# Layer 2 of a four-layer graph kernel: weight[l] w_ih^T multiplied out once per launch, and the state transposed at each step

**Chip, cores, metric.** One core of one Trainium2 chip.

## The reference, cut to what matters

64 graphs of 256 nodes with 256 features go through four layers. Each takes relu(layernorm(x)), and its result is added to x. Layer 0 is attention over 8 heads, layer 1 attention over one, layer 3 over four; layer 2 is a gated graph network of three steps with one pair of GRU matrices for all of them:

```python
A = (adj != 0).astype(x.dtype)
h = x                                             # relu(layernorm(x))
for i in range(3):
    m = einsum('bnd,de->bne', h, weight[i])       # 256 x 256
    aggr = einsum('bst,bsd->btd', A, m)           # A^T m
    gi = aggr @ w_ih.T + b_ih                     # 256 x 768
    gh = h @ w_hh.T + b_hh
    r = sigmoid(i_r + h_r); z = sigmoid(i_z + h_z)
    n = tanh(i_n + r * h_n)
    h = (1 - z) * n + z * h
```

Since aggr w_ih^T = A^T h (weight[i] w_ih^T), the product of the two matrices can be made once, and the multiplication by weight[i] goes out of the steps.

## The kernel before

All is in fp32. Two graphs, a pair, go through all layers together; up to three pairs are under way, some steps apart, so that one's matrix products fill another's softmax. A kernel line that says `yield` ends a step. The code's matmuls sum over the tiles' first axis, so there are two layouts: "T" tiles (features on partitions) and "token" tiles (nodes on partitions). The state hT is a T tile. psgm = h weight[l] makes a token tile m out of it, as a side effect of the multiplication:

```python
def layer2(xt, at, p):
    am = mask(f"am_{p}")
    ...
    hT = yield from norm_relu_T(xt, f"2_{p}")     # psn: transposes; then relu on ScalarE
    yield
    for l in range(NL):
        psm, psm4 = token_ps(f"psgm_{nm}")
        token_mm(gg_sb[:, l], hT, psm4)           # 8 matmuls of 128x256
        m = w4(f"m_{nm}")
        nc.scalar.copy(m, psm)
        yield
        psa = ...                                 # A^T m, 8 matmuls of 128x256
        aT = w4T(f"aT_{nm}")
        nc.scalar.copy(aT, psa)
        yield
        both = ((whhT, hT), (wihT, aT))
        r = sigmoid(0, "r")                       # psr: 8 matmuls of 128x512
        pshn = gate(((whhT, hT),), 4, "pshn")
        ...
        psin = gate(((wihT, aT),), 4, "psin")
        ...
        yield
        z = sigmoid(2, "z")                       # psz
        hnew = ...                                # named hg: n + z (h - n), GpSimd and VectorE
        hT = hnew
        yield
    ps, ps4 = token_ps(f"psx_{p}")                # psx: state to tokens, added to x
    for t in range(T):
        for k in range(2):
            nc.tensor.transpose(ps4[t][:, k*P:(k+1)*P], hT[:, k, t*P:(t+1)*P], ident)
    nc.vector.tensor_add(xt, ps, xt)
    yield
```

In layer 1, psf and psw are its projections, e its softmax numerators, wh the projected values divided by the sums, and psh<-wh,e the product of the two. psc and pso<-f,eT are the products of the softmaxes in layers 0 and 3.

## Time and profile before

| | before |
|---|---|
| time, median | 6370.52 us (3 runs, 6350.54 to 6373.97) |
| TensorE busy | 5787.0 us of 6365.3, 91% |
| TensorE idle | 578 us |
| mean granted clock of TensorE | 0.890 |
| a round (three pairs), mean of nine | 587.5 us |

The work repeats in rounds of three pairs, 10.67 of them. Slices, groups and one round of the timeline stand in the prediction. What TensorE waits for is in the view of its waits (tile, line, what it waited for: us in all, times, longest us); four of its lines:

```profile
PE psc L341 <- DVE pT L334: 143.6, 97, 4.7
PE psx L520 <- DVE hg L514: 88.9, 22, 6.8
PE psn L241 <- DVE xn L234: 44.6, 12, 5.2
PE psh L427 <- DVE wh L421: 18.7, 10, 6.6
```

psx waits long, twice in a round, for the new state hg. psh, the product of layer 1, hardly waits.

### The profile page before, as it was taken

The numbers are of one execution on the slowest core, as the hardware profiler recorded it, in microseconds if no ns is written. First come the engines' busy times: TensorE is split into PE (matmuls) and PEld (weight loads), VectorE is DVE, ScalarE is ACT, GpSimd is POOL, SyncE is SP. The second block draws the span as 40 slices with busy tenths as digits, with TensorE's granted clock in tenths as the row PEclk, the third lists the DMA queues.
The fourth block names the chain that finished last, engine by engine and source line by source line (L and its number), as shares of the span: only waits on it lengthen the run. The fifth ranks groups of instructions, "written<-read, shape, count | busy, mean of one in ns | idle before, by whom it ended". The sixth has DMA issues, their size and how long they took to land.

```text
span 6365.3 us, 60565 instructions
## 1 busy us (share of the span) xinstructions
PE 5787.0 (91%) x24500; PEld 3967.9 (62%) x24500; DVE 3090.6 (49%) x4479; ACT 2004.0 (31%) x4737; POOL 777.0 (12%) x582
## 2 busy tenths in 40 slices
PE   7998899889989988998899889889988998999887
PEld 6655765666566556655765665576557656665755
DVE  4435534554454445445544553554455345534534
ACT  2323322332233233223322332242233223322422
POOL 1011101100110111011001101110110011001011
PEclk7899799889978997898899889978987998899798
DMA  1000000000000000000000000000000000000000
GB/s 53 1 4 19 9 1 7 17 7 1 14 17 1 4 14 14 1 4 20 7 1 14 17 1 4 14 14 1 4 20 7 1 7 17 7 1 10 7 0 7
DMA packets 58279, 58.40 MB, mean 9 GB/s; under 512 B 4752, under 2 KB 58000, under 8 KB 58000
## 3 DMA queue, kind: packets, MB, share of 16 engines
q1 hardware_dynamic: 58000, 54.54, 2.6%
q8 instruction: 192, 3.15, 0.2%
q14 instruction: 87, 0.71, 0.0%
HBM read 37.76 MB, written 16.78 MB: 9 GB/s over the span
## 4 chain that ended last, share of the span: by engine, by line
PE 78%; DVE 13%; ACT 8%; issue 1%; DMA 0%; POOL 0%; SPq 0%; ACTq 0%; POOLq 0%; DVEq 0%
PE psr L475 10%; PE psz L475 10%; PE psc L341 9%; PE psin L475 5%; PE pshn L475 5%; PE psa L457 5%; PE pso L580 5%; PE psgm L250 4%; PE pssd L548 3%; PE pss L300 3%; DVE mx L260 3%; PE psq L278 2%; ACT s L262 2%; PE pso L250 2%; PE psf L536 2%; ACT eT L574 2%
## 5 line engine op out<-in xcount | busy, mean ns | idle before, releaser
L341 PE MATMUL psc<-v,pT 128*128 128x32 f32 x4096 | 621.6, 316 | 146.1 <-DVE pT L334 143.6
L341 PEld LDWEIGHTS psc<-v,pT 128*128 128x128 f32 x4096 | 612.1, 237 | 198.7 <-DVE pT L334 92.6
L262 ACT ACTIVATE s<-s,mx 128x256 f32<-128x256 f32 x1024 | 506.8, 499 | 304.5 <-DVE mx L260 166.0
L262 ACT ACTIVATE e<-e,mx 128x256 f32<-128x256 f32 x640 | 318.0, 500 | 630.6 <-DVE mx L260 630.5
L580 PE MATMUL pso<-f,eT 128*128 128x64 f32 x2048 | 323.1, 324 | 193.6 <-ACT eT L574 193.5
L580 PEld LDWEIGHTS pso<-f,eT 128*128 128x128 f32 x2048 | 302.8, 234 | 228.9 <-ACT eT L574 228.9
L307 DVE SCALAR_TENSOR_TENSOR s<-pss,mb 128x1024 f32<-128x1024 f32 x256 | 306.8, 1219 | 176.4 <-PE pss L300 176.4
L457 PE MATMUL psa<-am,m 128*128 128x256 f32 x1536 | 369.5, 396 | 2.3 <-ACT m L451 2.2
L475 PE MATMUL psz<-aT,wihT 128*128 128x512 f32 x768 | 363.6, 596 | 0.0
L475 PE MATMUL psr<-aT,wihT 128*128 128x512 f32 x768 | 363.3, 593 | 0.0
L475 PE MATMUL psin<-aT,wihT 128*128 128x512 f32 x768 | 345.2, 592 | 0.0
L457 PEld LDWEIGHTS psa<-am,m 128*128 128x128 f32 x1536 | 298.8, 199 | 47.6 <-ACT m L451 7.2
L327 PE MATMUL pst<-ident,s 128*128 128x128 f32 x2048 | 297.7, 307 | 18.7 <-DVE pT L334 14.5
L494 DVE TENSOR_SCALAR z<-z 128x1024 f32<-128x1024 f32 x96 | 66.6, 693 | 493.9 <-ACT z L491 493.9
L327 PEld LDWEIGHTS pst<-ident,s 128*128 128x128 f32 x2048 | 278.2, 163 | 32.8 <-DVE pT L334 17.1
L260 DVE TENSOR_REDUCE mx<-s 128x8 f32<-128x2048 f32 x128 | 292.0, 2281 | 1.2
L243 ACT ACTIVATE hT<-psn 128x1024 f32<-128x1024 f32 x128 | 130.9, 1022 | 488.8 <-PE psn L241 488.7
L348 DVE TENSOR_TENSOR ctxs<-psc,rz 128x256 f32<-128x256 f32 x128 | 54.4, 425 | 459.7 <-PE psc L341 459.7
L230 POOL TENSOR_SCALAR rs<-mv 128x4 f32<-128x4 f32 x128 | 33.7, 263 | 1973.1 <-DVE mv L228 1730.7
L475 PEld LDWEIGHTS psz<-aT,wihT 128*128 128x128 f32 x768 | 148.6, 194 | 191.0 <-issue 191.0
L250 PE MATMUL psgm<-gg_sb,hg 128*128 128x256 f32 x1024 | 254.4, 405 | 14.4 <-DVE hg L514 14.4
L594 POOL TENSOR_TENSOR x<-o,x 128x256 f32<-128x256 f32 x128 | 118.9, 929 | 1177.9 <-DVE o L588 1164.4
(140 smaller groups left out, 10040.8 us busy)
## 6 DMA issues: line engine op xcount, KB each, us to landing
x<-in_x_dram SPq DMA_DIRECT2D x32, 512.0 KB, 3.4
adj<-in_adj_dram SPq DMA_DIRECT2D x32, 512.0 KB, 3.3
out_dram<-x SPq DMA_DIRECT2D x32, 512.0 KB, 2.9
gg_sb<-in_L_gnn_weight_dram SPq DMA_DIRECT2D x3, 256.0 KB, 6.3
wih_sb<-in_L_gnn_w_ih_dram SPq DMA_DIRECT2D x1, 768.0 KB, 6.4
whh_sb<-in_L_gnn_w_hh_dram SPq DMA_DIRECT2D x1, 768.0 KB, 7.2
wq_sb<-in_L_gnn_Wq_dram SPq DMA_DIRECT2D x1, 256.0 KB, 5.4
wk_sb<-in_L_gnn_Wk_dram SPq DMA_DIRECT2D x1, 256.0 KB, 5.6
```

The costliest lines, as they stand in the source:

```text
L243: nc.scalar.activation(hT, ps, AF.Relu)
L250: mm(ps4[t], hT[:, k, t * P : (t + 1) * P], rhs[:, k, :], start=k == 0, stop=k == 1)
L260: nc.vector.tensor_reduce(mx, e, AX.X, ALU.max, negate=True)
L262: nc.scalar.activation(e[:, i, :], e[:, i, :], AF.Exp, bias=mx[:, i : i + 1], accum_out=zs[:, i : i + 1])
L300: mm(ps[:, j, cc * N : (cc + 1) * N], qT[r : r + D0, cc, t * P : (t + 1) * P], kT[r : r + D0, cc, g * N : (g + 1) * N], start=True, stop=True,
L307: nc.vector.scalar_tensor_tensor(s[:, 4 * half : 4 * half + 4, :], ps.rearrange("p a (b d) -> p (a b) d", d=N), SCALE, mb0[:, t : t + 1, : ...
L327: nc.tensor.transpose(psr[:, 2 * i + c, :], s[:, 4 * half + i, c * P : (c + 1) * P], ident)
L341: mm(ps[:, 0, h * D0 : (h + 1) * D0], pT[:, i, c, :], v[:, 2 * g + c, h * D0 : (h + 1) * D0], start=c == 0, stop=c == 1,)
L457: mm(psa[:, o, g * N : (g + 1) * N], m[:, 2 * g + c, o * P : (o + 1) * P], am[:, 2 * g + c, :], start=c == 0, stop=c == 1,)
L475: mm(ps[:, o, :], w[:, k, c0 : c0 + P], src[:, k, :], start=n == 0, stop=n == 2 * len(terms) - 1,)
L548: mm(ps[:, j, :], wdst_bc[:, k, 2 * half + j, :], hT[:, k, :], start=k == 0, stop=k == 1)
L580: mm(pso[:, 0, h * C3 : (h + 1) * C3], eT[:, 2 * h + c, :], f[:, 2 * g + c, h * C3 : (h + 1) * C3], start=c == 0, stop=c == 1,)
```

## The change

Its intent is to take 96 groups of psgm from TensorE, the engine that bounds the kernel, and to pay with 64 groups of transposes, which at full clock take 0.88 us each in the trace before, where a psgm takes 3.45. The first step of a pair needs none: the layernorm's tile is a token tile already and gets its relu in place. Cut to its core (removed comments, buffer lines and helper functions are left out):

```diff
+        for l in range(NL):                      # once per launch
+            transposed(ggT, gg_sb[:, l], D)
+            ... giT[:, l] = weight[l] @ w_ih.T
     def w4(name):
-        ... bufs=17
+        ... bufs=16
     def mask(name):
-        ... bufs=2
+        ... bufs=3
     def norm_relu_T(xt, nm, both=False):
+        if both:
+            nc.vector.tensor_scalar_max(xn, xn, 0.0)
         yield
         ...
-        return hT
+        return (hT, xn) if both else hT
     def layer2(xt, at, p):
-        hT = yield from norm_relu_T(xt, f"2_{p}")
+        hT, h = yield from norm_relu_T(xt, f"2_{p}", both=True)
         for l in range(NL):
-            psm, psm4 = token_ps(f"psgm_{nm}")
-            token_mm(gg_sb[:, l], hT, psm4)
-            m = w4(f"m_{nm}")
-            nc.scalar.copy(m, psm)
-            yield
-                            m[:, 2 * g + c, o * P : (o + 1) * P],
+                            h[:, 2 * g + c, o * P : (o + 1) * P],
-            both = ((whhT, hT), (wihT, aT))
+            both = ((whhT, hT), (giT[:, l], aT))
             ...
             hT = hnew
             yield
+            if l < NL - 1:
+                ps, ps4 = token_ps(f"psh2_{nm}")
+                to_tokens(hT, ps4)
+                h = w4(f"h_{nm}")
+                nc.scalar.copy(h, ps)
+                yield
```

The profile shows psh2 as psh<-ident,hg; psh<-wh,e is the product of layer 1.

More of the change, by code (lines that the diff above doesn't have):

```diff
@@ L98, in tile_adj_preln_d4 @@
     wo_sb = load_w("wo_sb", wo)
-    gg_sb = const.tile([P, NL, 2, D], FP, name="gg_sb")
-    for l in range(NL):
-        nc.sync.dma_start(gg_sb[:, l], ggw[l].rearrange("(k p) o -> p k o", p=P))
     def row_bcast(dst, vec):
@@ L117, in tile_adj_preln_d4 @@
     row_bcast(b3a_bc[:, 0:D], b3)
-    wihT = const.tile([P, 2, 3 * D], FP, name="wihT")
+    giT = const.tile([P, NL, 2, 3 * D], FP, name="giT")
     whhT = const.tile([P, 2, 3 * D], FP, name="whhT")
@@ L142, in transposed @@
                     nc.vector.tensor_copy(dst[:, k, o * P : (o + m) * P], ps[:, 0, 0 : m * P])
+        gg_sb = prep.tile([P, NL, 2, D], FP, name="gg_sb")
+        for l in range(NL):
+            nc.sync.dma_start(gg_sb[:, l], ggw[l].rearrange("(k p) o -> p k o", p=P))
+        wihT = prep.tile([P, 2, 3 * D], FP, name="wihT")
         for w, wT, nm in ((w_ih, wihT, "wih_sb"), (w_hh, whhT, "whh_sb")):
@@ L147, in tile_adj_preln_d4 @@
             transposed(wT, t, 3 * D)
+        HALF = 3 * D // 2
+        for l in range(NL):
+            ggT = prep.tile([P, 2, D], FP, tag="ggT", bufs=2, name=f"ggT_{l}")
+            transposed(ggT, gg_sb[:, l], D)
+            for f in range(2):
+                ps = bank2(f"gi_{l}_{f}")
+                for half in range(2):
+                    for k in range(2):
+                        mm(
+                            ps[:, half, 0:HALF],
+                            ggT[:, k, f * P : (f + 1) * P],
+                            wihT[:, k, half * HALF : (half + 1) * HALF],
+                            start=k == 0,
+                            stop=k == 1,
+                        )
+                nc.scalar.copy(giT[:, l, f, :].rearrange("p (h e) -> p h e", h=2), ps[:, :, 0:HALF])
         nc.vector.tensor_add(brz, bih_sb[:, 0:4], bhh_sb[:, 0:4])
@@ L208, in w4 @@
     def w4(name):
-        return work.tile([P, T, D], FP, tag="w4", bufs=17, name=name)
+        return work.tile([P, T, D], FP, tag="w4", bufs=16, name=name)
     def w4T(name):
@@ L218, in mask, with to_T, to_tokens, norm_relu_T @@
     def mask(name):
-        return work.tile([P, T, N], FP, tag="mask", bufs=2, name=name)
-    def norm_relu_T(xt, nm):
+        return work.tile([P, T, N], FP, tag="mask", bufs=3, name=name)
+    def to_T(src, ps):
+        for k in range(2):
+            for t in range(T):
+                nc.tensor.transpose(ps[:, k, t * P : (t + 1) * P], src[:, t, k * P : (k + 1) * P], ident)
+    def to_tokens(src, ps4):
+        for t in range(T):
+            for k in range(2):
+                nc.tensor.transpose(ps4[t][:, k * P : (k + 1) * P], src[:, k, t * P : (t + 1) * P], ident)
+    def norm_relu_T(xt, nm, both=False):
         st = small.tile([P, T, 6], FP, tag="st", name=f"st_{nm}")
@@ L236, in norm_relu_T @@
             )
+        if both:
+            nc.vector.tensor_scalar_max(xn, xn, 0.0)
         yield
         ps = bank2(f"psn_{nm}")
-        for k in range(2):
-            for t in range(T):
-                nc.tensor.transpose(ps[:, k, t * P : (t + 1) * P], xn[:, t, k * P : (k + 1) * P], ident)
+        to_T(xn, ps)
         hT = work.tile([P, 2, N2], FP, tag="hT", bufs=4, name=f"hT_{nm}")
         nc.scalar.activation(hT, ps, AF.Relu)
-        return hT
+        return (hT, xn) if both else hT
     def token_mm(rhs, hT, ps4):
@@ L503, in layer2 @@
                 )
-            psin = gate(((wihT, aT),), 4, "psin")
+            psin = gate(((giT[:, l], aT),), 4, "psin")
             nc.vector.tensor_add(hn, psin, hn)
@@ L516, in layer2 @@
             yield
+            if l < NL - 1:
[4 more added lines that the diff above has]
+                yield
         ps, ps4 = token_ps(f"psx_{p}")
-        for t in range(T):
-            for k in range(2):
-                nc.tensor.transpose(ps4[t][:, k * P : (k + 1) * P], hT[:, k, t * P : (t + 1) * P], ident)
+        to_tokens(hT, ps4)
         nc.vector.tensor_add(xt, ps, xt)
```

## The prediction

> **What bounds the kernel now.** I read the page first: busy times, slices, chain of waits.
>
> ```profile
> PE 5787.0 (91%) x24500; PEld 3967.9 (62%) x24500; DVE 3090.6 (49%) x4479; ACT 2004.0 (31%) x4737; POOL 777.0 (12%) x582
> PEclk7899799889978997898899889978987998899798
> PE 78%; DVE 13%; ACT 8%; issue 1%; DMA 0%; POOL 0%; SPq 0%; ACTq 0%; POOLq 0%; DVEq 0%
> ```
>
> TensorE bounds the kernel, and 78% of the chain that ended last is TensorE work. But 13% of its 91% lies beside someone else's link of the chain: removing such work gives nothing. The clock dips to 0.7 once in every round of three pairs of graphs (some 587 us: the third psx of a round starts at 1167.9, that of the next at 1754.7). Then the groups of TensorE by shape:
>
> ```profile
> L250 PE MATMUL psgm<-gg_sb,hg 128*128 128x256 f32 x1024 | 254.4, 405 | 14.4 <-DVE hg L514 14.4
> L250 PE MATMUL psgm<-gg_sb,hT 128*128 128x256 f32 x512 | 138.8, 433 | 0.0
> L520 PE MATMUL psx<-ident,hg 128*128 128x128 f32 x256 | 43.4, 325 | 88.9 <-DVE hg L514 88.9
> ```
>
> psgm is what goes: 254.4 + 138.8 = 393.2 us busy. psx is the same sort of transposes that come: 43.4 / 256 = 0.17 us each. Each psgm matmul shows as two records, each transpose as one. In the chain of waits psgm has 4.0% of the span, 255 us, so about a third of psgm is already hidden. Last, the timeline of TensorE in one round (start, length; idle before it in brackets):
>
> ```profile
> 970.71 1.88 PE L475 MATMUL psz<-aT,wihT 128*128 128x512 f32 x4
> 972.43 3.62 PE L250 MATMUL psgm<-gg_sb,hg 128*128 128x256 f32 x16
> 975.88 3.62 PE L427 MATMUL psh<-wh,e 128*128 128x256 f32 x16
> 979.33 1.04 PE L520 MATMUL psx<-ident,hg 128*128 128x128 f32 x8
> ...
> 1075.71 3.62 PE L250 MATMUL psgm<-gg_sb,hg 128*128 128x256 f32 x16
> 1080.64 1.06 PE L520 MATMUL psx<-ident,hg 128*128 128x128 f32 x8 [1.31 <-DVE hg L514]
> ...
> 1167.89 1.94 PE L520 MATMUL psx<-ident,hg 128*128 128x128 f32 x8 [6.78 <-DVE hg L514]
> 1169.62 1.91 PE L241 MATMUL psn<-ident,xn 128*128 128x128 f32 x8
> ```
>
> Around 972, psgm fills the time in which layer 1's softmax is made for psh: no wait. At 1075.71 it fills most of the 4.9 us that z and the new state take on ScalarE and VectorE: only 1.31 us remain. At 1167.89 nothing fills: 6.78 us idle[...].
>
> [...]after 6.78 us idle 8 transposes take 1.9 us, against 1.04 elsewhere, and the next psq 6.28 us where psk of the same size takes 3.60. [...]Full clock: 16 psgm records 3.45 us, 8 transposes 0.88 us, so a factor of 3.9 for as many output elements[...] Of the same shape, z<-z takes 0.693 us and the tensor_tensor hg 1.22[...]the new maximum should cost 0.69 us.
>
> **The change, part by part.** There are 32 pairs, 10.67 rounds.
> *TensorE:* out go 96 psgm, 393 us. In come 2 × 32 × 8 = 512 transposes, 512 × 0.17 = 87 us. Busy time falls by 306 us: were the idle time unchanged, 6370 - 306 = 6064.
> *Preparation:* 12 transposes and 24 matmuls of 128x384. The same kind at full clock: psr, 8 matmuls of 128x512, takes 6.87 us, so 24 × 0.86 × 0.75 = 15.5; transposes 1.6; waits for copies between them some 4. 21 us, all before the first psn, so all on the path.
> *Other engines:* VectorE gets 32 × 0.69 = 22 us; ScalarE loses 32 of 96 copies of 1.01 us. A third mask buffer frees VectorE from waits on psa (97.6 + 80.2 us), but these fall into stretches in which TensorE is full, so I count nothing. DMA moves the same weights.
>
> *Where the wait moves.* I compiled the changed kernel and read the order of instructions, without times. I then put the durations of the trace on one round:
>
> a) From psc before the round's first psgm (805.1) to the second step's psr (884.0). The first psgm goes; psa moves into the wait for layer 1's softmax. The new transposes stand right behind psz, psn and pss and wait some 2.6 us for the state. Layer 1's psh is ready at 865.8 as against 866.5 (bounded by VectorE), but 4.7 us of psa no longer stand behind it: gain 5.6 us.
> b) psr at 884.0 to psr at 925.3: psgm 3.45 and psgm 3.69 with its wait of 1.31 go, one set of transposes 0.9 and a wait of 0.6 come; psm moves out (0.9), psct in (counted in a): gain 6.2.
> c) To psr at 983.8. Psh now stands behind psf, psw, psx, psa, no more behind psz and psgm. From the end of psw, VectorE does half of e, x, e, e, mx with statistics between, ScalarE 2.1 us of exponentials, VectorE rz and wh: 10.3 us. TensorE has psx 0.9 and psa 3.45 to do: it waits 6.0 us where it waited 0. Sum of the pieces: 63 us against 58.5: loss 4.5.
> d) To psr at 1030.4: psgm 3.45 goes, another becomes transposes (3.45 - 0.9): gain 5.9.
> e) To psr at 1089.2: before psx at 1080.64 only 0.9 us of transposes remain as cover, and VectorE's order now puts two passes over e between z and the new state, 2.45 us: psx comes at 1083, after 6.5 us idle: loss 2.5.
> f) The psgm at 1125: 3.45 - 0.9: gain 2.55.
>
> Sum 5.6 + 6.2 - 4.5 + 5.9 - 2.5 + 2.55 = 13.3 us a round. [...]after the one at 1167.89 about 3 us of matmul were lost. I count 2 + 3 + 1 = 6 us a round. That leaves 7 to 13 us a round, 75 to 140 us, less 21 for preparation: a gain of 55 to 120 us. By the busy time it would be 285.
>
> **Rivals.**
> 1. *The whole 306 us come through, less preparation: 6085.* For it: TensorE is 91% busy, 100% between 925 and 984. Against it: the chain shows a third of psgm hidden, which caps the gain at 255 - 45 - 21, or 190 us (6180).
> 2. *The removed psgm was cover; new waits at psh and psx and a halved clock eat it: 6250 to 6315.* For it: the compiled order, and the wait of 6.78 us at 1167.89, which is what psx without cover looks like. Against it: I placed the pieces by hand; 2 us at one place of the round shift the sum by 21.
> 3. *VectorE becomes the bound or clocks fall in the dense stretch too: 6350 or more.* VectorE is at 49% and gets 22 us; transposes already stand among dense matmuls (psn at 997.40, 16 in 1.91 us, full clock). Unlikely.
>
> **Range and chances.** Mostly rival 2, with some weight on rival 1 capped by the chain: 6275 us, 6170 to 6360 eight times in ten. The line of 2% lies at 6243, between the cap (6180) and my middle: faster 0.35, same 0.62, slower 0.03.
>
> **What would show it.** Psgm gone; new transposes 70 to 90 us busy; TensorE about 5500 us busy, more if the clock halves oftener; its share of the span falling to 87 or 88%. In the waits: psh for wh up from 18.7 us to 60 to 100, psx for hg from 88.9 to 130 to 145, a new wait of the state's transposes for hg of about 30. Slow psh or psa behind those waits, mean clock at or below 0.89. First psn at 50 us in place of 29.4. I am wrong if psh and psx wait no longer than before (then 6100 to 6200), or if the round of 587 us shrinks by over 15 us.

Passages that no trace of this case shows are cut from it, and marked. A gain of 13.3 us a round, less 6 for the clock, is 7.3, taken as 7 to 13 (from the whole clock term to none); in 10.67 rounds and less 21 us of preparation that gave the gain of 55 to 120 us. The 6 us are my estimate. It starts from the about 3 us that I put down as lost at 1167.89, after 6.78 us idle, where psx took 1.94 us in place of 1.04 and the next psq 6.28 where psk took 3.60 (granted clock 0.50 and 0.57), and carries that over to the waits of 6.0 us in c), 6.5 in e) and 3.9 in a) as 2, 3 and 1 us; that such a loss follows waits of these lengths is an assumption. The 0.69 us of the new maximum is the measured length of z<-z, of the same shape.

## More of the kernel before

The metric is the device time of one execution in microseconds (us), as the median of the runs.

In which order TensorE gets the matmuls of the three pairs is set when the kernel is compiled: a scheduler arranges the steps' instructions, and the source gives only a part of that order.

## The result

| | before | after |
|---|---|---|
| time, median of 4 runs | 6366.73 us (6350.54 to 6373.97) | 6389.67 us (6387.44 to 6393.66) |
| ratio | | 1.0048, 95% interval 1.0029 to 1.0067 |
| TensorE busy | 5787.0 us | 5630.3 us |
| TensorE idle | 578 us | 755 us |
| mean granted clock | 0.890 | 0.867 |
| first psn starts at | 29.43 us | 48.60 us |
| a round, mean of nine | 587.5 us | 589.0 us |

A ratio here and below is the mean time of one kernel's fast runs over that of the other's fast runs of the same rounds, so it is not quite the ratio of the medians quoted. The time lies above the predicted range, and it is slightly slower: the interval leaves out 1. The changed kernel is correct.

From the page after: busy times and the chain of waits.

```profile
PE 5630.3 (88%) x23536; PEld 3818.6 (60%) x23536; DVE 3115.1 (49%) x4517; ACT 1974.8 (31%) x4711; POOL 793.8 (12%) x582
PE 77%; DVE 13%; ACT 7%; issue 1%; POOL 0%; DMA 0%; SPq 0%; ACTq 0%; POOLq 0%; DVEq 0%
```

The groups by shape (busy us, mean ns | idle us just before), and the waits:

```profile
L457 PE MATMUL psh<-wh,e 128*128 128x256 f32 x512 | 167.6, 499 | 113.7 <-DVE wh L451 113.7
L249 PE MATMUL psh<-ident,hg 128*128 128x128 f32 x512 | 76.8, 300 | 50.2 <-DVE hg L539 50.2
L249 PE MATMUL psx<-ident,hg 128*128 128x128 f32 x256 | 53.1, 377 | 136.8 <-DVE hg L539 136.8
```

```profile
PE psx L249 <- DVE hg L539: 136.8, 22, 6.8
PE psc L371 <- DVE pT L364: 115.3, 97, 4.5
PE psh L457 <- DVE wh L451: 113.7, 22, 6.6
PE psn L243 <- DVE xn L268: 78.8, 11, 7.8
PE psh L249 <- DVE hg L539: 50.2, 22, 3.9
```

psgm is gone, 393.2 us of it. The new transposes take 76.8 us, the products in the preparation 16.2 and its 12 transposes about 2, so busy time should have fallen by 298 us. It fell by 157. The other 141 us are, on balance, old matmuls that got longer: psh<-wh,e 167.6 us (121.6 before), psa 276.2 + 136.0 (369.5 before), psr 28 us more, psf<-hT,wa_bc 79.6 (61.1 before), psx 53.1 (43.4 before). (Some of this had been hidden in psgm: 96 groups at the full-clock 3.45 us would be 331 us, so by this estimate 62 of its 393 were slow clock: the one at 859.70 took 6.10 us, at a granted clock of 0.60. That what stands in its place inherits this is not shown.) And idle time grew by 177 us: psh<-wh waits 113.7 us (18.7), psx 136.8 (88.9), the new transposes 50.2, psn 78.8 (44.6); against that, psc waits 28 us less and psgm's 14 are gone.

Where that happens shows in TensorE's timeline of one round (start, length, and in brackets the idle time before). The first place is where the prediction's step c) stands, the second e), the third the psx that the prediction showed at 1167.89:

```profile
978.69 1.04 PE L249 MATMUL psh<-ident,hg 128*128 128x128 f32 x8
...
985.63 3.62 PE L482 MATMUL psa<-am,h 128*128 128x256 f32 x16
994.83 6.64 PE L457 MATMUL psh<-wh,e 128*128 128x256 f32 x16 [5.58 <-DVE wh L451]
1001.30 1.88 PE L500 MATMUL psr<-hg,whhT 128*128 128x512 f32 x4
...
1008.17 3.60 PE L500 MATMUL pshn<-hg,whhT 128*128 128x512 f32 x8
...
1087.32 1.04 PE L249 MATMUL psh<-ident,hg 128*128 128x128 f32 x8
1094.20 1.94 PE L249 MATMUL psx<-ident,hg 128*128 128x128 f32 x8 [5.84 <-DVE hg L539]
1095.94 5.52 PE L482 MATMUL psa<-am,h 128*128 128x256 f32 x16
...
1187.02 1.94 PE L249 MATMUL psx<-ident,hg 128*128 128x128 f32 x8 [6.78 <-DVE hg L539]
```

Two things are to be seen. After each of these waits the next matmuls run wholly or in part at half the clock: psh takes 6.64 us in place of 3.62 (mean granted clock 0.54), psx 1.94 in place of 1.04 (0.50, both times) and psa behind it 5.52 in place of 3.62 (0.64). And behind the waiting psh stands psr<-hg,whhT, which reads the state hg: that is ready, since the transposes at 978.69 read the same hg. It starts 12 us after psa has ended (985.63 + 3.62 = 989.25), when psh is through; between 989.25 and psh's start at 994.83 this trace has no matmul. I looked at this second thing too late.

### The profile page after: what moved, and what is told of

Read it like the earlier page. It is cut to its first block, busy times and chain, and to the rows that moved or that the text cites. A ratio compares the mean times of both kernels' runs of the same rounds, so it can differ in the third digit from the quotient of the medians.

```text
span 6385.7 us, 58549 instructions
## 1 busy us (share of the span) xinstructions
PE 5630.3 (88%) x23536; PEld 3818.6 (60%) x23536; DVE 3115.1 (49%) x4517; ACT 1974.8 (31%) x4711; POOL 793.8 (12%) x582
## 4 chain that ended last, share of the span: by engine, by line
PE 77%; DVE 13%; ACT 7%; issue 1%; POOL 0%; DMA 0%; SPq 0%; ACTq 0%; POOLq 0%; DVEq 0%
PE psr L500 11%; PE psz L500 11%; PE psc L371 9%; PE psa L482 6%; PE psin L500 5%; PE pshn L500 5%; PE pso L609 5%; PE pssd L577 3%; PE psh L457 3%; PE pss L330 2%; PE psq L308 2%; DVE mx L290 2%; DVE s L337 2%; ACT eT L603 2%; PE psf L565 2%; ACT e L292 2%
## 5 line engine op out<-in xcount | busy, mean ns | idle before, releaser
L500 PE MATMUL psr<-aT,giT 128*128 128x512 f32 x768 | 373.5, 610 | 0.0
L500 PE MATMUL psz<-aT,giT 128*128 128x512 f32 x768 | 362.5, 595 | 0.0
L500 PE MATMUL psin<-aT,giT 128*128 128x512 f32 x768 | 345.3, 592 | 0.0
L357 PE MATMUL pst<-ident,s 128*128 128x128 f32 x2048 | 313.5, 318 | 19.6 <-ACT wh L436 13.9
L357 PEld LDWEIGHTS pst<-ident,s 128*128 128x128 f32 x2048 | 293.7, 170 | 33.3 <-ACT wh L436 16.3
L519 DVE TENSOR_SCALAR r<-r 128x1024 f32<-128x1024 f32 x96 | 66.7, 695 | 481.0 <-ACT r L516 481.0
L516 ACT ACTIVATE z<-psz,brz 128x512 f32<-128x512 f32 x192 | 121.5, 684 | 576.5 <-PE psz L500 576.5
L482 PE MATMUL psa<-am,h 128*128 128x256 f32 x1024 | 276.2, 429 | 1.1 <-ACT h L546 1.1
L457 PE MATMUL psh<-wh,e 128*128 128x256 f32 x512 | 167.6, 499 | 113.7 <-DVE wh L451 113.7
L500 PEld LDWEIGHTS psr<-aT,giT 128*128 128x128 f32 x768 | 150.4, 196 | 192.1 <-issue 183.6
```

Of the source, the lines that this page charges most:

```text
L357: nc.tensor.transpose(psr[:, 2 * i + c, :], s[:, 4 * half + i, c * P : (c + 1) * P], ident)
L457: mm(ps4[t], e[:, 2 * g + cj, ci * P : (ci + 1) * P], wh[:, 2 * g + cj, :], start=cj == 0, stop=cj == 1,)
L482: mm(psa[:, o, g * N : (g + 1) * N], h[:, 2 * g + c, o * P : (o + 1) * P], am[:, 2 * g + c, :], start=c == 0, stop=c == 1,)
L500: mm(ps[:, o, :], w[:, k, c0 : c0 + P], src[:, k, :], start=n == 0, stop=n == 2 * len(terms) - 1,)
L519: nc.vector.tensor_scalar(s, s, 0.5, 0.5, ALU.mult, ALU.add)
```

## The experiments

The first theory was the prediction's own: psgm had covered waits, and without cover TensorE idles at psh and psx and its clock halves. The rivals: the new maximum (it stands on VectorE's path to psn), the third mask buffer, and the missing step (psa comes one step earlier). Sixteen kernels ran; all gave correct results. Each batch had its own runs of the kernel before, with medians of 6365.0 to 6368.7 us. Against it and by the 2% limit, 1, 2, 4, 6, 8 and 10 are "same", 14 is "unclear" and the others are "faster"; every interval leaves out 1.

### 1. The maximum in a tile of its own

In place, the maximum has to end before psn may read xn.

```diff
-            nc.vector.tensor_scalar_max(xn, xn, 0.0)
+            h = w4(f"h0_{nm}")
+            nc.vector.tensor_scalar_max(h, xn, 0.0)
...
-        return (hT, xn) if both else hT
+        return (hT, h) if both else hT
```

> The changed kernel, but the maximum (relu) of the tokens goes to a tile of its own, so that the transposes psn of layer 2 no longer wait for it; the same work on every engine. Theory of new waits: psn's wait for xn falls from 78.8 us to 40 to 50 (before: 44.6), time 6340 to 6375 against the changed kernel's 6390. Rival, the new maximum costs as load on VectorE: 6390 as it is.

Measured: 6335.59 us (6335.21 to 6336.03), ratio to before 0.9956 (0.994 to 0.9973). psn's wait for xn fell from 78.8 to 42.3 us. So the maximum costs 54 us of what the change lost, and I had counted 22 us of VectorE work for it, off the path. It isn't the main part: TensorE's busy time fell by 25 us only, and the waits of psh and psx stayed. (TensorE's order is not quite the same: once in a round a psc is interleaved with psa in another way.)

### 2. A step back between transposes and psa

```diff
         for l in range(NL):
             nm = f"{p}_{l}"
+            if l == 0:
+                yield
             psa = bank2(f"psa_{nm}")
```

> The changed kernel with one step boundary (a yield, no instruction) put back at layer 2's first iteration, where the removed psgm had one; a pair then has 43 steps as before and the compiled order of TensorE has layer 1's psh behind psz and the state's transposes again, as in the kernel before. Theory that the order moved by the lost step costs the gain: psh's wait for wh falls from 113.7 us to 20 to 50, the stretch from psr of step 0 of the second pair to psr of its step 1 falls from 65.5 to about 57 us, time 6250 to 6300. Rival, the missing cover alone costs it whatever the order: within 20 us of 6390.

Measured: 6341.4 us (6334.2 to 6361.18), ratio 0.997. psh's wait fell to 68.3 us and the stretch of step c) from 65.5 to 56.9 us, as expected; but the stretch ahead of it, from the third psx of a round to the end of b), grew from 338.9 to 345.9 us. (The trace is of the slowest of the four runs.) The step's place was a cause at c), and most of that was given back elsewhere; the time met neither the theory's 6250 to 6300 us nor the rival's 6390.

### 3. Useless matmuls in the waits

Eight matmuls, 3.45 us, into the tile that psh or psx overwrites afterwards:

```diff
         ps, ps4 = token_ps(f"psh_{p}")
+        token_mm(wq_sb, hT, ps4)
...
-            hT = hnew
+            hprev, hT = hT, hnew
...
         ps, ps4 = token_ps(f"psx_{p}")
+        token_mm(wq_sb, hprev, ps4)
```

> The changed kernel with 512 useless matmuls of 128x256 (64 groups of the size of psgm, 3.45 us each at full clock, 221 us in all) written into psh's and psx's banks ahead of their real work, from operands that are ready early; the results are overwritten. Theory that TensorE idles there with its clock halved: they fall into the waits at psh and psx and keep the clock up; mean clock rises from 0.867 to 0.88 or more, time 6360 to 6440. Rival, TensorE's busy time sets the end: 6390 + 221 = 6610.

Measured: 6212.06 us (6208.68 to 6227.91), ratio 0.9767, clock 0.893. With 64 x 3.45 = 221 us of useless work it is 178 us faster than the changed kernel, and far below the 6360 to 6440 that I had expected. I took it for the clock: a wait filled keeps TensorE at full speed. That reading didn't hold (see 12 and 13).

### 4. Only the buffers

The kernel before with 3 masks and 16 token tiles. (The changed kernel with the old numbers doesn't build: it deadlocks, so the third mask is part of the change.)

> The kernel before with the changed kernel's buffers (3 masks in place of 2, 16 token tiles in place of 17), nothing else. Both theories: VectorE's waits of the masks on psa (97.6 + 80.2 us) go, TensorE was full there, so within 10 us of the kernel before (6367). If the third mask had moved the order or the time, over 20 us either way.

Measured: 6399.29 us (6396.85 to 6408.66), ratio 1.0059 (1.0044 to 1.0074). A miss: 34 us slower, though TensorE's tiles start in the same order (only how a psc is interleaved with psr and with psq differs, once each in a round) and its waits are the same to within 5 us; busy rose from 5787.0 to 5822.2 us and the clock fell from 0.890 to 0.884. Why is open, and whether the changed kernel, which has these buffers, pays the same is not shown.

### 5. Transposes as filler

```diff
-        token_mm(wq_sb, hT, ps4)
+        for _ in range(3):
+            to_tokens(hT, ps4)
```

and likewise with hprev ahead of psx: 24 transposes, 2.6 us.

> As the run that filled the waits with useless matmuls (6212 us), but the filling is transposes: 24 of 128x128 in each of 64 places, from the same ready operands into the same banks; the compiled order around psh is the same. Theory that the clock is what the matmul filling bought: [...]mean clock stays at or below 0.87, psh stays at 5 to 6.6 us in the places where it was slow, time 6370 to 6450. Rival, the filling helped by the order or by keeping TensorE from idling as such: 6200 to 6260, clock 0.89.

Measured: 6186.4 us (6182.86 to 6192.71), ratio 0.9715, clock 0.892. That is a little below the rival's band; matmuls aren't needed as filler. The less filler, the faster: that should have made me doubt the clock at once.

### 6. The kernel before with the filler of 3

> The kernel before with the same useless matmuls ahead of psh and psx. There psgm covers these places already, but for the third psx of a round (6.8 us idle). If filling is a gain only where the change opened waits: 6367 + 10.67 x (5 x 3.45 - 3 to 8 us) = 6430 to 6520 (if only one place of six gains). If filling is good in general, whatever the change: below 6300.

Measured: 6459.33 us (6451.22 to 6471.02), ratio 1.0145. The filler as such isn't good. But "it helps only where the change opened waits" was one more reading that run 14 undid.

### 7. Filler of 3, and the maximum apart

> Both cures together: useless matmuls ahead of psh and psx (6212 us) and the maximum in a tile of its own (54 us gained on the changed kernel). The two waits stand in different places of the round, so the gains should add: 6150 to 6180. If they overlap, 6200 or more.

Measured: 6178.88 us (6168.02 to 6185.85), ratio 0.9701. The maximum gives 33 us here in place of 54.

### 8. psx a step later

Kernel of 1, with a `yield` ahead of psx.

> No useless work: the maximum in a tile of its own (6336 us), and a step boundary ahead of psx, so that the compiled order has psa and psh of other pairs ahead of psx. Theory of the waits: psx's wait falls from 136.8 us to about 70 (only the third psx of a round is left), its halved clock goes with it, psh for wh stays near 114: 6336 - 10.67 x (6 + 3) = 6240, give or take 40. Rival, the wait only moves to another instruction: within 20 us of 6336.

Measured: 6337.06 us (6333.2 to 6340.93), ratio 0.9951: nothing gained on kernel 1. Its waits:

```profile
PE psh L249 <- DVE hg L541: 143.2, 43, 5.8
PE psx L249 <- DVE hg L541: 19.1, 11, 1.7
```

psx waits 19.1 us in place of 136.8, but the new transposes 143.2 in place of 50.2. A step of the source is too coarse a unit: it moved the same wait to the next instruction that needs the same hg.

### 9 to 11. Filler at one place, or with the maximum apart

Filler of 24 transposes: 9 is kernel 5 with the edit of 1; 10 has it ahead of psh alone, 11 ahead of psx alone.

> The changed kernel with 24 filler transposes ahead of psh and of psx, and the maximum in a tile of its own. Matmuls as filler gained 178 us alone and 211 with the maximum apart (33 more); transposes alone gained 203. Theory: the two act at different places, so 6145 to 6165 us here, the best of the series. Rival: the shorter filler leaves the wait of psn to show again, so that both together give no more than the filler alone, 6180 to 6190.

> 24 filler transposes ahead of psh alone. By the lengths of the pieces of a round, psh and the slow pieces behind it made up about 3.5 us at one place and 5 us at the other (psr of the second step behind half-clock psc), the third psx 8.3: if the places are independent and both matter, 6290 +- 30 us here. Rival: all of the gain comes from psx and its new place in the order, and this run stays at 6370 to 6400.

> 24 filler transposes ahead of psx alone; the compiler also puts the real psx behind psa or behind pso there, as in the run with both fillers. Both places matter: 6290 +- 30 us, and this gain and that of the run with filler at psh alone add up to some 200 us. Rival, that psx is all: 6190 to 6210.

Measured: 6162.6 us (6161.54 to 6196.61), 6280.81 (6277.21 to 6290.32) and 6207.83 (6199.66 to 6220.99); ratios 0.9693, 0.9868, 0.9755. Both places count: 109 us at psh, 182 at psx. That makes 291, but both at once gave 203. Run 11 came out where its rival, "psx is all", had put it, and not at 6290; run 10 rules that rival out.

### 12. A filler too short to fill

```diff
-        for _ in range(3):
+        for _ in range(1):
             to_tokens(hT, ps4)
```

> Only 8 filler transposes (0.9 us) at both places. The compiled order moves psx and psh at least as far back as with 24. If the new order is what helped, the gain stays: 6210 us or less. If the filler helps by keeping TensorE's clock up through a wait of 5 to 7 us, 0.9 us of it leaves over 4 us idle and the clock falls as before: 6300 us or more, clock below 0.88.

The fall "as before" is what the trace after shows: 4.63 us of idle time ahead of psh, then a granted clock of 0.71.

Measured: 6064.23 us (6063.65 to 6067.89), ratio 0.9527 (0.9513 to 0.9541). That is 122 us faster than with 24 transposes and 325 faster than the changed kernel. 0.9 us can't bridge a wait of 5 to 7 us, so "filled waits keep the clock up" is out as the explanation. What the compiled kernels show is another order of TensorE's instructions: with 8 transposes, psh stands behind the next pieces of layer 0 and the first matmuls of psr, and the third psx stands in psq.

### 13. The order alone

One single transpose at each place (0.11 us from its start to that of the next matmul), in a tile that is overwritten. I compared the compiled order first: TensorE's tiles start in exactly the order of 12. (Inside psr and psh, and inside psn and pst, some matmuls are interleaved otherwise in the traces.)

```diff
         ps, ps4 = token_ps(f"psh_{p}")
+        nc.tensor.transpose(ps4[0][:, 0:P], hT[:, 0, 0:P], ident)
...
-            hT = hnew
+            hprev, hT = hT, hnew
...
         ps, ps4 = token_ps(f"psx_{p}")
+        nc.tensor.transpose(ps4[0][:, 0:P], hprev[:, 0, 0:P], ident)
```

> The changed kernel with one single filler transpose (0.11 us) ahead of psh and of psx: compiled, TensorE's order is identical to the run with 8. If the order alone did it, 6015 to 6070 us, TensorE about 5490 to 5540 us busy, the waits of psx for hg and psh for wh near zero. If the filler's time is needed to bridge waits, over 6200 us.

Measured: 6054.7 us (6042.79 to 6063.88), ratio 0.9512 (0.9484 to 0.954), clock 0.887. That is 49 us less filler than in 12 and 9.5 us less time, so some of the filler of 12 had fallen into idle time. The page and the waits:

```profile
PE 5504.9 (91%) x23600; PEld 3718.4 (62%) x23600; DVE 3111.4 (52%) x4517; ACT 1971.4 (33%) x4711; POOL 793.6 (13%) x582
```

```profile
PE pso L611 <- ACT eT L605: 183.0, 125, 6.5
PE psc L371 <- DVE pT L364: 125.4, 106, 5.0
PE psn L243 <- DVE xn L268: 80.5, 11, 10.2
PE psh L249 <- DVE hg L540: 50.6, 22, 4.2
```

psx and psh for wh have gone from the top of the list; the other long waits are within some 10 us of those after the change, and psa now waits 15.3 us for the copied tokens h (1.1 before). Their groups, with 2.4 and 0.1 us of idle time where it was 136.8 and 113.7:

```profile
L458 PE MATMUL psh<-wh,e 128*128 128x256 f32 x512 | 117.5, 383 | 0.1
L249 PE MATMUL psx<-ident,hg 128*128 128x128 f32 x256 | 36.6, 291 | 2.4 <-DVE hg L540 2.4
```

And the same three places of a round in the timeline:

```profile
1497.13 1.04 PE L249 MATMUL psh<-ident,hg 128*128 128x128 f32 x8
...
1504.18 3.62 PE L483 MATMUL psa<-am,h 128*128 128x256 f32 x16
1507.64 0.27 PE L454 MATMUL psh<-ident,hT 128*128 128x128 f32 x1
1507.75 1.88 PE L501 MATMUL psr<-hg,whhT 128*128 128x512 f32 x4
1509.47 1.88 PE L501 MATMUL psr<-aT,giT 128*128 128x512 f32 x4
1511.18 1.88 PE L501 MATMUL psr<-hg,whhT 128*128 128x512 f32 x4
1512.99 3.69 PE L458 MATMUL psh<-wh,e 128*128 128x256 f32 x16
1516.52 1.88 PE L501 MATMUL psr<-aT,giT 128*128 128x512 f32 x4
1518.24 3.60 PE L501 MATMUL pshn<-hg,whhT 128*128 128x512 f32 x8
...
1597.39 1.04 PE L249 MATMUL psh<-ident,hg 128*128 128x128 f32 x8
...
1599.82 3.72 PE L483 MATMUL psa<-am,h 128*128 128x256 f32 x16 [1.28 <-ACT h L547]
1603.37 1.04 PE L603 MATMUL pst<-ident,e 128*128 128x128 f32 x8
1604.25 1.04 PE L249 MATMUL psx<-ident,hg 128*128 128x128 f32 x8
...
1684.53 3.54 PE L308 MATMUL psq<-hT,wq_sb 128*128 128x512 f32 x4
1687.90 1.04 PE L249 MATMUL psx<-ident,hg 128*128 128x128 f32 x8
```

psr starts right behind psa and runs in the time in which psh waited; psh comes when wh is there, at full speed (3.69 us). psx stands behind psa and pst, or in the midst of psq. From the transposes to pshn it is 1518.24 - 1497.13 = 21.1 us, in place of 1008.17 - 978.69 = 29.5. At four such places of a round (a psh of the same kind, from psa to pshn, is the fourth: 19.2 in place of 30.6) the difference sums to 36 us; the round shrank by 34, from 589.0 to 555.3 us.

### 14. The same order for the kernel before

The edit of 13 in the kernel before.

> The kernel before with the same single transposes, so psx and psh stand behind ready work there too. It had 88.9 us of waits for psx and 18.7 for psh, and slow matmuls behind the third psx: 120 to 180 us less, 6190 to 6250 us, if order is what costs. Then the change would be worth some 180 us at equal order. Rivals: the gain is the same 305 us as in the changed kernel (then the change is worth nothing even so), or none (then the order matters only where the change took the cover away, 6350 to 6400).

Measured: 6237.4 us (6228.97 to 6262.48), ratio 0.9801 (0.9771 to 0.9831). 131 us less: psx waits 14.6 us in place of 88.9. So the kernel before had the same fault, and suffered less from it. With the same edit in both, the change is worth 6237.4 - 6054.7 = 183 us, or 2.9%. It also sheds light on 6: 6237.4 + 221 us of filler is 6458, and 6459.33 was measured, although that kernel's order isn't quite the same.

### 15. The order and the maximum apart

Kernel 13 with the edit of 1.

> Order loosened and the maximum in its own tile. The wait of psn for xn with its slow clock was worth 54 us alone, 33 and 24 with fillers: 6020 to 6040 us if e13 is near 6060, the best of all. Rival: nothing, since the order is another one.

Measured: 6016.15 us (6013.07 to 6018.56), ratio 0.9447 (0.9426 to 0.9467): the fastest of all, 39 us below 13; psn's wait for xn is 58.6 us in place of 80.5.

### 16. The order of psx alone

> Single transpose ahead of psx alone: psx goes behind psq in one place and behind psa in another, psh stays. 24 transposes there gave 182 us; without 16 to 23 of them (2.6 us x 32 = 83 us busy, part hidden): 6140 to 6190 us. Then psh's order has the remaining 80 to 130 us. Rival: psx's gain was the clock, 6300 or more.

Measured: 6206.66 us (6198.71 to 6217.65), ratio 0.9747, slightly above what was expected; psx's wait gone, psh's at 109.8 us. So psx's place is worth 183 us and psh's another 152. Run 11, with 24 transposes there, took 6207.83 us: the filler's length didn't show, though the orders of the two differ in some places, and psh waited 75.9 us there.

| | changed kernel | with psx's order | with psx's and psh's | and the maximum apart |
|---|---|---|---|---|
| us | 6389.67 | 6206.66 | 6054.7 | 6016.15 |
| TensorE busy, us | 5630.3 | 5575.4 | 5504.9 | 5477.9 |
| TensorE idle, us | 755 | 633 | 536 | 533 |
| clock | 0.867 | 0.878 | 0.887 | 0.892 |

## Why the prediction was wrong

**What held.** Psgm gone, the new transposes 76.8 us (70 to 90 said), psx for hg 136.8 us (130 to 145), TensorE's share 88% (87 or 88), the first psn at 48.6 us (50), the mean clock below 0.89. Step d) gained 6.0 us a round (5.9 said). Rival 2 had the direction right as the kernel stands: the waits did move to psh and psx. Beyond what was said went psh's wait for wh (113.7 us, 60 to 100 said), that of the new transposes (50.2, about 30 said) and the busy time (5630 us, about 5500 said).

**What failed.** The stretches of a round by the prediction's marks, mean of nine rounds, in us:

| step | predicted, before the clock | measured |
|---|---|---|
| ahead of a), from the third psx | nothing counted | loss 1.4 |
| a) and b) | gain 11.8 | gain 3.9 |
| c) | loss 4.5 | loss 7.0 |
| d) | gain 5.9 | gain 6.0 |
| e) | loss 2.5 | loss 3.7 |
| f) | gain 2.55 | gain 0.7 |
| clock, all steps | loss 6 | in the rows above |
| sum | gain 7.3 | loss 1.5 |

c) to f) are right to within 2 us each once the clock is put in (2 us at c, 3 at e). The step that failed is a). With its 1 us for the clock the gain of a) and b) was 10.8 us, and it measured 3.9; with the 1.4 lost ahead of them that is 8.3 of the 8.8 us by which the sum missed, and 8.8 us in 10.67 rounds are 94 us of the time. From the end of psc to pshn of the second step, a) had a gain of 5.6 us; the kernel is 3.0 slower there (87.9 us against 84.9). From that pshn to the end of b) it gains 7.0 (27.3 against 34.3), about what b) said. Two terms of a) were wrong, and one wait lies ahead of it.

First, "Layer 1's psh is ready at 865.8 as against 866.5 (bounded by VectorE)". It comes later, since the softmax that it waits for starts from TensorE's psf and psw, and these are late. Before, then after:

```profile
846.33 1.88 PE L396 MATMUL psf<-hT,wa_bc 128*128 128x512 f32 x4
866.47 3.69 PE L427 MATMUL psh<-wh,e 128*128 128x256 f32 x16 [0.67 <-DVE wh L421]
...
862.06 1.94 PE L249 MATMUL psh<-ident,hg 128*128 128x128 f32 x8 [3.81 <-DVE hg L539]
863.79 3.62 PE L426 MATMUL psf<-hT,wa_bc 128*128 128x512 f32 x4
885.26 5.12 PE L457 MATMUL psh<-wh,e 128*128 128x256 f32 x16 [4.63 <-DVE wh L451]
```

The new transposes wait 3.81 us, not 2.6, and psf behind them runs at half the clock (3.62 us in place of 1.88, granted clock 0.50). The end of psc is at 805.05 before and 820.14 after. Counted from there psw ends at 46.6 us before and 50.9 after, and psh starts at 61.4 and 65.1 (65.3 in the mean); 60.8 was predicted. That is 4.5 of the 8.6 us by which a) missed; the rest lies between psh and pshn.

Second, the clock behind psh. I had a wait of 3.9 us and counted 1 us. The wait was 4.63 us, psh took 5.12 us instead of 3.62 (granted clock 0.71), and psr behind it, mixed with psc, took 13.8 us from its start to pshn (0.63). Alone it takes 6.9 (1008.17 - 1001.30) and psc at full clock 1.9, so by this estimate 5.0 us are the clock's. That makes 6.5 us with psh's own 1.5. Not all of it is new: from psh to pshn the granted clock was halved for 13.1 us after and for 6.8 us before, where it fell on psc and psa.

Third, psn, ahead of a). It waits for the new maximum, whose 0.69 us of work I had counted, but not its place in VectorE's order, behind a pass over scores: 78.8 - 44.6 = 34 us more, or 3.2 us a round. (At 805.77 it had waited 6.63 us and took 1.94 us in place of 1.04, at a granted clock of 0.50.) The stretch as a whole lost 1.4. Run 1 puts all that the maximum cost, wherever it showed, at 54 us.

**Readings that don't hold.** I had read the clock as low without a break behind the psx at 1167.89; by the granted clock in that trace it was half until 1171.8 us, full to 1175.2 and half again to 1182.0. The prediction finds a factor of 3.9 between psgm and the transposes; but each output element of psgm takes two matmuls, as it sums over 256 features. Per matmul and column the factor is 2.0 (3.45 us for 8 of 256 columns, 0.88 for 8 of 128); the other factor of 2 is psgm's second matmul. The next third psx starts at 1754.3, not 1754.7. None of this moves the sum.

**Where the middle was set.** The sum gave a gain of 55 to 120 us; I put the middle at 95, with some weight on rival 1. With the measured 2.5 us up to the end of b) in its place the same sum is 2.5 - 4.5 + 5.9 - 2.5 + 2.55 - 5 = -1.05 us a round, which with the preparation is a loss of 32 us; 23 came.

**What I did not ask.** I had read the compiled order and taken it as given. "Psh now stands behind psf, psw, psx, psa, ... it waits 6.0 us" was right, and the next question was missing: what stands behind psh, and is it ready? Psr was. My rival 1, "the whole 306 us come through", I had given up because of the waits. With two instructions of 0.11 us that let the compiler put ready work ahead, busy time fell by 5787.0 - 5504.9 = 282 us from that before (298 less 17 that the 64 single transposes show, at 0.27 us each), idle time by 42, and the time is 6054.7 us; the prediction's figure for unchanged idle time was 6064. Of that, though, 131 us are to be had without the change (run 14), so that 6054.7 lies so near to 6064 is chance. And "psgm was cover" is right only with an addition: it was cover at those places because nothing that was ready had been put there.

**Clock or order?** Both are in the numbers, and the change of order in 13 moved both. From the changed kernel to 13 the span fell by 345 us: 219 of idle time and 125 of busy time, the latter being, on balance, matmuls that no longer run at half the clock (mean granted clock 0.867 and 0.887). In the trace after, 4.63 and 5.58 us of idle time were followed by psh at 5.12 and 6.64 us (granted clock 0.71 and 0.54); without such a wait, in the traces before and of 13, it takes 3.62 to 3.69. The filler runs, which I had read as a remedy for the clock, brought a looser order along; runs 12, 13 and 16 show that the order gives as much or more without the filling.

**Open.** Why the scheduler puts psh and psx ahead of ready work, and why a single transpose in their tile changes that, was not found out; whether the order can be had without it neither. That both fillers of 24 give less than the sum of the two alone is in line with their order being another than 12's, which no run isolates. The 34 us of run 4 are unexplained; if the changed kernel pays them too, they are a part of its loss that no run isolates. Psn's wait, 58.6 us, and that of pso for eT, 190.4 us, are left in the fastest version.

## What to carry to other kernels

When work is taken from the engine that bounds a kernel and the time doesn't move, look at each new wait for what stands behind it in that engine's queue: if it is ready, try another order before you blame the work or the change (here the order was worth 335 us of 6390 with the change and 131 of 6369 without: runs 13 and 14). An experiment that adds instructions may change the compiled order as well; compare the order before you read the result, and shrink the added work to nearly nothing as a control. And compare a change with the kernel before at equal order, else one is credited with the other.
